# First attention: keys of two blocks by seven products in place of eight

## The chip, the cores and the metric

The kernel runs on one core of a Trainium2 chip. The metric is the device time of one execution in microseconds (us); of several runs the median is taken. The engines are called PE (matrix products), DVE (vector), ACT (activations), POOL (GpSimd) and SP (here only a queue that issues DMAs). PE writes to PSUM, eight banks of 512 columns of fp32 in 128 partitions; everything else lies in SBUF.

## The reference

A network of six layers works on x, 128 rows of 256. The first layer, the only one that the change touches, is an attention of these rows over a context of M = 12544 rows:

```
q = (layernorm(x) @ Wq)           in 4 heads of 64
k, v = context @ Wkv              in 4 heads of 64
attn = softmax(where(mask, q k^T / 8, -inf))
x = x + (attn v) @ Wo
```

Then follow a gated delta net, a layer of experts, a second attention over the same context with 16 heads, a linear attention with decay, and a second layer of experts. All is fp32.

## The kernel before

The context comes transposed, so that its 256 columns lie in the partitions (two halves, index k). It is cut into 24 blocks of 512 rows and a last one of 256 (`BLOCKS`), and each block stays in SBUF in a place of its own (`ctx_blocks[b][:, k, :]`), because the second attention uses it again.

`xattn0_first` (L365) is the first layer. For each block of the context it makes

- keys, transposed (`keys`, L414): kT[:, m, :] for the two halves m of the 256 key columns, each the sum of two products (k = 0, 1) of a 128x128 quarter of Wk with a 128x512 half of the block. So a block takes four products of 128x128 by 128x512. A product in fp32 is two passes of PE, which the profile counts as two instructions;
- values (`values`, L426): eight products with 256 columns;
- scores (`scores`, L449): per 256 rows of the block ("a part"), 16 products into a tile `st` of two banks; DVE adds minus a maximum that was estimated from block 0 (`nm`) and writes `e` (L466), ACT takes the exponential in place (L467), POOL casts the mask to fp32 (`mk`, L469), and POOL, or DVE for the second part of every odd block, multiplies `e` by it (L475);
- `add_up` (L478): DVE adds `e` into `sums`, the denominators;
- `weigh` (L482): PE adds values times `e` into `ot`, which stays in one PSUM bank over the whole layer.

Blocks are taken in pairs (loop at L561). PE's, ACT's and DVE's order is written out by hand (`manual_schedule`); POOL's and SP's is made by a scheduler when the kernel is built. In a pass b > 0 of the loop the order is: values of b-2 and add_up of b-2, values of b-1 and add_up of b-1, keys of b and b+1, weigh of b-2 and b-1, scores of b and b+1. A pair's keys, values and scores go through one ring of three PSUM tiles of two banks each (`two`, L411); `ot` has the seventh bank, and `spare`, into which PE multiplies zeros at the start, has the eighth. `e` has five buffers, the cast masks two.

The scores of the first pair come before that, with the layer norm, the queries and the estimate of the maximum: L541 to L552. While the layer norm waits for other engines, PE makes keys and values of block 0 (`between`).

In the last pass there is one block, 24. `filler` gives PE products of the second attention there (its lines are L1063, keys, and L1084, values), and from then on through the delta net and the experts, so that PE has work while other engines are slow. The filler's total work is fixed.

Weights of later layers are loaded ahead through a ring of four buffers (`ring`, `weights`, L83): Wq, then the four tiles of the delta net's projections in the passes that hold blocks 4, 6, 8 and 10 (`ahead`). All of these loads, the blocks of the context and the masks (L452) are issued on SP's queue.

## Time and profile before

| what | value |
|---|---|
| median of 3 runs | 753.38 us (752.00 to 753.56) |
| the profiled execution | 752.12 us |
| its span, first to last instruction | 750.3 us |
| mean granted clock of PE | 0.993 |
| PE busy in 102.9 to 124.3 us | 21.40 of 21.40 us |
| DVE busy there | 13.06 us |
| ACT busy there | 8.28 us |
| POOL busy there | 10.41 us |
| scores of the first pair on PE | from 20.8 us |
| last weigh of block 23 on PE ends | 271.8 us |

The span is what the profiler shows between the first and the last instruction; the time of the execution is 1.8 us longer. The first attention takes the first 286 us of it. In a group's line stand the source line, the engine, the operation, the tiles written and read (out<-in), the shape and the number of instructions, then the time they were busy in us and the mean of one in ns, then the idle time of the engine just before them and what ended it. A line of the timeline begins with start and length in us; "x4" means four instructions in a row, with their whole length. POOL stands for GpSimd, PEld for PE's loading of weights.

### The profile page before, as it was taken

What the parts mean: (1) busy time and instruction counts of PE and PEld (TensorE: products, weight loads), DVE (VectorE), ACT (ScalarE), POOL (GpSimd) and SP (SyncE); (2) the same over time, 40 slices, a digit from 0 to 9 for tenths busy, and PEclk for the clock granted to TensorE, in tenths of its full rate; (3) what the DMA queues carried; (4) which work ended last, traced back from release to release, by engine and by line L of the source; (5) the groups of instructions that cost most, each with busy time, mean ns of one, the idle gap of its engine ahead of it and who ended that gap; (6) DMA issues with size and microseconds to landing.
All of it is one profiled execution on the core that took longest, in us unless ns stands there. A gap on an engine that the chain in (4) does not pass through costs nothing.

```text
span 750.3 us, 23185 instructions
## 1 busy us (share of the span) xinstructions
PE 733.4 (98%) x10472; PEld 561.4 (75%) x10472; DVE 300.6 (40%) x482; ACT 390.9 (52%) x480; POOL 177.9 (24%) x178
## 2 busy tenths in 40 slices
PE   8999999999999999999999999999999999999985
PEld 4678877777787777666677666668888888888873
DVE  2675556656655555983123251001111111111155
ACT  2434433334344333573235223337789999999931
POOL 5555444455554420506012030000000000000000
PEclk9999999999999999999999999999999999999998
DMA  9980000000000002224111344113652222222000
GB/s 318 385 294 4 9 5 9 8 8 8 8 5 3 1 29 93 94 99 141 46 44 43 126 85 127 74 67 100 158 120 78 69 63 74 74 60 73 6 2 12
DMA packets 36124, 56.66 MB, mean 76 GB/s; under 512 B 5904, under 2 KB 12608, under 8 KB 36016
## 3 DMA queue, kind: packets, MB, share of 16 engines
q1 hardware_dynamic: 35648, 54.05, 23.2%
q8 instruction: 84, 1.38, 0.8%
q0 software_dynamic: 368, 1.03, 0.4%
q14 instruction: 24, 0.20, 0.1%
HBM read 42.09 MB, written 12.98 MB: 73 GB/s over the span
## 4 chain that ended last, share of the span: by engine, by line
PE 92%; ACT 5%; issue 1%; DVE 1%; POOL 0%; ACTq 0%; DVEq 0%; POOLq 0%
PE pv L439 12%; PE pk L1063 11%; PE pv L1084 11%; PE pk L420 11%; PE one L1158 10%; PE st L460 6%; PE ot L489 6%; PE st_a L1143 5%; PE st_b L1143 5%; ACT es L1149 2%; ACT w L1149 2%; PE pr L672 1%; PE one L1143 1%; PE py L992 1%; ACT e L1149 1%
## 5 line engine op out<-in xcount | busy, mean ns | idle before, releaser
L475 POOL TENSOR_TENSOR e<-e,mk 128x1024 f32<-128x1024 f32 x37 | 87.4, 2361 | 130.7 <-issue 116.9
L1143 PE MATMUL one<-qs,ks 32*128 32x128 f32 x784 | 108.1, 282 | 0.0
L1190 DVE TENSOR_TENSOR ctx<-ctx,one 128x512 f32<-128x512 f32 x47 | 32.3, 687 | 163.9 <-PE one L1158 163.9
L1158 PE MATMUL one<-e,ctx 128*17 128x128 f32 x784 | 94.7, 275 | 0.0
L1143 PEld LDWEIGHTS one<-qs,ks 32*128 32x128 f32 x784 | 94.2, 187 | 0.0
L1063 PE MATMUL pk<-ctx,wk 128*128 128x512 f32 (+1 forms) x200 | 92.6, 589 | 0.0
L1084 PE MATMUL pv<-wv,ctx 128*128 128x256 f32 x384 | 90.0, 382 | 0.6 <-ACT kh L1070 0.6
L439 PE MATMUL pv<-wkv,ctx 128*128 128x256 f32 x392 | 88.4, 383 | 0.0
L1084 PEld LDWEIGHTS pv<-wv,ctx 128*128 128x128 f32 x384 | 71.8, 190 | 21.0 <-issue 10.7
L420 PE MATMUL pk<-ctx,wkv 128*128 128x512 f32 (+1 forms) x200 | 86.5, 584 | 0.0
L467 ACT ACTIVATE e<-e 128x1024 f32<-128x1024 f32 x49 | 51.8, 1057 | 64.5 <-DVE e L466 61.1
L439 PEld LDWEIGHTS pv<-wkv,ctx 128*128 128x128 f32 x392 | 73.3, 190 | 10.9
L1158 PEld LDWEIGHTS one<-e,ctx 128*17 128x17 f32 x784 | 73.1, 98 | 6.2 <-issue 0.2
L466 DVE TENSOR_TENSOR e<-st,nm 128x1024 f32<-128x1024 f32 x49 | 56.7, 1218 | 50.1 <-PE st L460 50.1
L1158 PE MATMUL one<-es,ctx 128*17 128x128 f32 x1776 | 74.8, 275 | 0.0
L1149 ACT ACTIVATE es<-st_a 128x1536 f32<-128x1536 f32 x49 | 70.9, 1446 | 0.0
L420 PEld LDWEIGHTS pk<-ctx,wkv 128*128 128x128 f32 x200 | 37.9, 190 | 41.4 <-issue 39.7
L1149 ACT ACTIVATE e<-one 128x512 f32<-128x512 f32 x98 | 58.9, 601 | 17.7 <-PE one L1143 14.9
L1070 ACT ACTIVATE kh<-pk,col 128x512 f32<-128x512 f32 (+1 forms) x50 | 33.8, 678 | 63.7 <-PE pk L1063 62.7
L480 DVE TENSOR_TENSOR sums<-sums,e 128x1024 f32<-128x1024 f32 x49 | 63.1, 1287 | 5.7 <-POOL e L475 3.6
L1158 PEld LDWEIGHTS one<-es,ctx 128*17 128x17 f32 x1776 | 60.5, 98 | 0.1
L1143 PE MATMUL st_a<-qs,ks 32*128 32x128 f32 x1176 | 57.6, 283 | 1.6 <-issue 1.6
(339 smaller groups left out, 1049.7 us busy)
## 6 DMA issues: line engine op xcount, KB each, us to landing
ctx<-in_ctxT SPq DMA_DIRECT2D x24, 512.0 KB, 9.2
kd<-kh SPq DMA_DIRECT2D x48, 256.0 KB, 2.0
ks<-kd SPq DMA_DIRECT2D x192, 64.0 KB, 2.9
w<-in_L_ffn_expert_w SPq DMA_DIRECT2D x4, 512.0 KB, 3.8
ctx<-in_L_ffn_We SPq DMA_DIRECT2D x4, 512.0 KB, 7.2
msk<-in_maskT SPq DMA_DIRECT2D x24, 64.0 KB, 1.9
w<-in_L_attn_Wqk SPq DMA_DIRECT2D x2, 768.0 KB, 10.1
w<-in_L_attn_Wv SPq DMA_DIRECT2D x2, 768.0 KB, 12.0
```

The source lines that it names most:

```text
L420: nc.tensor.matmul(pk[:, m, :n], wkv[:, k, m * 128 : (m + 1) * 128], ctx_blocks[b][:, k, :], start=(k == 0), stop=(k == KC - 1),)
L439: nc.tensor.matmul(pv[:, i, c * D : (c + 1) * D], ctx_blocks[b][:, k, rows], wkv[:, k, D:], start=(k == 0), stop=(k == KC - 1),)
L460: nc.tensor.matmul(st[:, 2 * q + m, c, :], kTs[b][rows, m, (c0 + c) * 128 : (c0 + c + 1) * 128], qT[rows, m, :], start=True, stop=True,)
L466: nc.vector.tensor_add(e, st, nm.unsqueeze(2).to_broadcast([128, 4, 2, S]))
L467: nc.scalar.activation(e, e, AF.Exp)
L475: engine.tensor_mul(e, e, mk.unsqueeze(1).to_broadcast([128, 4, 2, S]))
L480: nc.vector.tensor_add(sums, sums, e)
L1063: nc.tensor.matmul(pk, wk1[:, k, m * 128 : (m + 1) * 128], ctx_blocks[b][:, k, :], start=(k == 0), stop=(k == KC - 1),)
L1084: nc.tensor.matmul(pv[:, c, :], ctx_blocks[b][:, k, rows], wv1[:, k, :], start=(k == 0), stop=(k == KC - 1),)
L1143: nc.tensor.matmul(three[:, j - 1, g, :] if j else one[:, 0, g, :], kss[b % 3][r, g // 2, g % 2, c * 128 : (c + 1) * 128], qs[r, g, :], st ...
L1149: nc.scalar.activation(e.rearrange("p j g s -> p (j g s)"), st.rearrange("p j g s -> p (j g s)"), AF.Exp)
L1158: nc.tensor.matmul(one[32 * j : 32 * j + DH + 1, 0, g, :], v[:, c, 8 * (g // 2) + 2 * j + g % 2, :], e3[:, j - 1, g, :] if j else e1[:, 0, ...
```

## The change

Only `xattn0_first` changes.

Keys of two whole blocks b and b+1 are made together (`seven`), for the eleven pairs from block 2 on. The two blocks are taken as a matrix of quarters a11, a12 (block b, halves k) and a21, a22 (block b+1), Wk as w11, w12, w21, w22; the product of two matrices of two by two quarters is made with seven products of quarters in place of eight, from sums of the quarters. The sums of weights, `tw`, are made once by POOL at the start; the four sums of the context, s1 to s4, are made by POOL for each pair one pass ahead (`add_context`). They lie in two buffers of the ring `ring` and in `places[0]`, two sets in turn. Each of the seven products is one of PE's with its own bank; ACT copies the first into kT of block b, and DVE adds the others to what is there already, SBUF plus PSUM into SBUF, seven adds of 512 columns in all. Keys of blocks 0, 1 and 24 stay as they were.

PSUM is now handed out in single banks: seven in turn (`Banks`), and `ot` in the eighth, zeroed at the very start, where PE's products of zeros also go. So values and keys have a copy for each bank, and the scores of a part have two banks, `st[0]` and `st[1]`, with an add on DVE for each (four heads' halves, 128x512).

The order on PE, ACT and DVE within a pass is written as a string: v is a step of values (four products with 256 columns), k one of the seven products with its copy or adds, a an add into `sums`, m DVE's own mask product, w the weighing of a part, f a step of filler. The mask product of DVE, until now emitted with the scores, thus stands behind a first add.

From POOL's queue as built: in a pass of the steady state POOL has the casts of the first two masks, then the four context sums for the next pass's keys, then mask product, cast, mask product, cast, mask product. At the start it has the weight sums, the conversion of block 0's mask, five DMA issues, the context sums of blocks 2 and 3 and of 4 and 5, among them two small rows (`turned`) and two casts, then the first mask product. On SP's queue the two loads of L0_attn_Wv stand behind the last mask's load now; before, they stood among the loads of the context.

```diff
-            tc.tile_pool(name="x0_mm", bufs=3, space=PSUM) as ps_mm,
+            tc.tile_pool(name="x0_mm", bufs=1, space=PSUM) as ps_mm,
...
+            ot = ot_bank[:, : 2 * S].rearrange("p (m s) -> p m s", m=2)
+            nc.tensor.matmul(ot_bank[:, : 2 * S], zeros[:, :128], zeros[:, : 2 * S], start=True, stop=False)
...
+            tw = wp.tile([128, 4, 128], F32, name="tw")
+            w11, w12, w21, w22 = [wkv[:, k, m * 128 : (m + 1) * 128] for k in range(2) for m in range(2)]
+            nc.gpsimd.tensor_sub(tw[:, 0], w12, w11)
+            nc.gpsimd.tensor_sub(tw[:, 1], w22, tw[:, 0])
+            nc.gpsimd.tensor_sub(tw[:, 2], w22, w12)
+            nc.gpsimd.tensor_sub(tw[:, 3], w21, tw[:, 1])
+            room = [ring.tile([128, 1536], F32, tag="w", name="w") for _ in range(2)]
+            slots = [r[:, i * 512 : (i + 1) * 512] for r in room for i in range(3)]
+            slots += [places[0][:, i * 512 : (i + 1) * 512] for i in range(2)]
...
+            class Banks:
+                def __init__(self, n):
+                    self.left = cycle(range(n))
+                def one(self, name):
+                    i = next(self.left)
+                    return (ps_mm if i else ps_ot).tile([128, 512], F32, tag=f"b{i}", name=name)
...
+            banks, few = Banks(7), Banks(7)
+            next(few.left)
+            def add_context(b):
+                s1, s2, s3, s4 = slots[b // 2 % 2 :: 2]
+                a11, a12 = [ctx_blocks[b][:, k, :] for k in range(2)]
+                a21, a22 = [ctx_blocks[b + 1][:, k, :] for k in range(2)]
+                nc.gpsimd.tensor_add(s1, a21, a22)
+                nc.gpsimd.tensor_sub(s2, s1, a11)
+                nc.gpsimd.tensor_sub(s3, a11, a21)
+                nc.gpsimd.tensor_sub(s4, a12, s2)
+                sums_of[b] = (a11, a12, s4, a22, s1, s2, s3)
+            def seven(b):
+                a11, a12, s4, a22, s1, s2, s3 = sums_of.pop(b)
+                for i in range(2):
+                    kTs[b + i] = kvp.tile([128, 2, 512], F32, tag="kT", name="kT")
+                c11, c12, c21, c22 = [kTs[b + i][:, m, :] for i in range(2) for m in range(2)]
+                for left, right, sums in (
+                    (a11, w11, ()),
+                    (s2, tw[:, 1], ((c12, c11),)),
+                    (a12, w21, ((c11, c11),)),
+                    (s3, tw[:, 2], ((c21, c12),)),
+                    (s1, tw[:, 0], ((c22, c21), (c12, c12))),
+                    (a22, tw[:, 3], ((c21, c21),)),
+                    (s4, w22, ((c12, c12),)),
+                ):
+                    p = banks.one("pk")
+                    nc.tensor.matmul(p, right, left, start=True, stop=True)
+                    if not sums:
+                        nc.scalar.copy(c11, p)
+                    for out, to in sums:
+                        nc.vector.tensor_add(out, to, p)
+                    yield
...
-                    e = ep.tile([128, 4, 2, S], F32, tag="e", name="e")
-                    nc.vector.tensor_add(e, st, nm.unsqueeze(2).to_broadcast([128, 4, 2, S]))
-                    nc.scalar.activation(e, e, AF.Exp)
...
+                st = [banks.one("st").rearrange("p (m c s) -> p m c s", m=2, c=2) for _ in range(2)]
...
+                for q in range(2):
+                    of = slice(2 * q, 2 * q + 2)
+                    nc.vector.tensor_add(
+                        e[:, of], st[q], nm[:, of].unsqueeze(2).to_broadcast([128, 2, 2, S])
+                    )
+                nc.scalar.activation(e, e, AF.Exp)
...
+                if b % 2 == 0 or c0 == 0:
+                    mask(b, c0 // 2)
+            def mask(b, i):
+                engine = nc.vector if b % 2 and i else nc.gpsimd
+                engine.tensor_mul(es[b][i], es[b][i], bys.pop((b, i)))
+            def add_up(e):
+                nc.vector.tensor_add(sums, sums, e)
...
+            add_context(2)
             for b in range(0, NB, 2):
...
-                    for c in (b - 2, b - 1):
-                        if c > 0:
-                            values(c)
-                        add_up(c)
-                    for c in pair:
-                        keys(c)
-                    weigh(b - 2, False)
...
+                    k = seven(b) if len(pair) == 2 else keys(b)
+                    v = chain(values(b - 2) if b > 2 else (), values(b - 1))
+                    order = "v v a0 m3 k k a1 v k k a2 v k k k a3 w0 w1 w2 w3"
+                    if b == 2:
+                        order = "m3 a0 v k k a1 v k k a2 k k k a3 w0 w1 w2 w3"
+                    elif len(pair) == 1:
+                        order = "v v a0 m3 k a1 v k a2 v a3 w0 w1 f f f w2 w3"
+                        filler.into(few, "mm")
...
+                    if b + 3 < NB:
+                        add_context(b + 2)
                 for c in pair:
-                    scores(c)
+                    for c0 in range(0, BLOCKS[c][1] // 128, 2):
+                        scores(c, c0)
```

## The prediction

> **What bounds the kernel now.** I read the busy shares first, then the chain of work in order of time, then the timeline of one period of the first attention, then the groups whose durations I need.
>
> The busy shares of the page:
>
> ```profile
> PE 733.4 (98%) x10472; PEld 561.4 (75%) x10472; DVE 300.6 (40%) x482; ACT 390.9 (52%) x480; POOL 177.9 (24%) x178
> ```
>
> PE is busy in 98% of the span: what it is spared counts, as long as nothing else makes it wait. The chain of work in order of time (start, length, what), one period of the first attention and the start of the next:
>
> ```profile
> 102.98 3.77 PE st L460 x64
> 106.75 7.10 PE pv L439 x32
> 113.86 6.87 PE pk L420 x16
> 120.72 3.65 PE ot L489 x64
> 124.37 3.77 PE st L460 x64
> ```
>
> The period is 3.77 + 7.10 + 6.87 + 3.65 = 21.39 us without a gap. A product of keys is two passes, 6.87 / 16 = 0.43 us each, so 0.86 us. What DVE and POOL do in a period, from the timeline (start, length, engine, line):
>
> ```profile
> 61.35 4.62 DVE L466 TENSOR_TENSOR e<-st,nm 128x1024 f32<-128x1024 f32 x4 [4.59 <-PE st L460]
> 63.80 2.37 POOL L475 TENSOR_TENSOR e<-e,mk 128x1024 f32<-128x1024 f32 x1 [10.71 <-issue]
> 66.26 0.40 POOL L469 TENSOR_SCALAR mk<-msk 128x256 f32<-128x256 uint8 x1
> 66.63 2.36 POOL L475 TENSOR_TENSOR e<-e,mk 128x1024 f32<-128x1024 f32 x1
> 69.07 0.41 POOL L469 TENSOR_SCALAR mk<-msk 128x256 f32<-128x256 uint8 x1
> 69.44 2.35 POOL L475 TENSOR_TENSOR e<-e,mk 128x1024 f32<-128x1024 f32 x1
> 69.51 3.36 DVE L475 TENSOR_TENSOR e<-e,mk 128x1024 f32<-128x1024 f32 x1 [3.54 <-POOL mk L469]
> 71.88 2.59 POOL L469 TENSOR_SCALAR mk<-msk 128x256 f32<-128x256 uint8 x2
> 72.80 5.33 DVE L480 TENSOR_TENSOR sums<-sums,e 128x1024 f32<-128x1024 f32 x4
> ```
>
> Two things are to be seen. DVE's last mask product (69.51) lasts 3.36 us: it starts with POOL's (69.44 to 71.79) and ends 1.08 after it, so it did nothing until POOL was done. Then POOL's two casts take 2.59 in place of 2 x 0.40, while DVE adds up: the two engines take turns, instruction by instruction. But the adds of L466, whose source is a PSUM tile, run at their usual pace while POOL works from 63.80 on. DVE ends at 78.13 and has idle time until the next scores; all of this is hidden now.
>
> Durations that I need, from the groups, from the answer on line 948, and from DVE's timeline in which two instructions follow each other:
>
> ```profile
> L1190 DVE TENSOR_TENSOR ctx<-ctx,one 128x512 f32<-128x512 f32 x47 | 32.3, 687 | 163.9 <-PE one L1158 163.9
> L480 DVE TENSOR_TENSOR sums<-sums,e 128x1024 f32<-128x1024 f32 x49 | 63.1, 1287 | 5.7 <-POOL e L475 3.6
> ```
>
> ```profile
> L948 POOL TENSOR_TENSOR o<-o,sg x3: 1266/1267/1657, 396.8 to 400.4; 128x512 f32<-128x512 f32 x3
> ```
>
> ```profile
> 15.60 0.69 DVE L541 CUSTOM_DVE_ANT_0 t<-sc,mb 128x512 f32<-128x512 f32 x1 [5.11 <-PE sc L538]
> ...
> 16.21 0.69 DVE L541 CUSTOM_DVE_ANT_0 t<-sc,mb 128x512 f32<-128x512 f32 x1
> ```
>
> L1190 has the form of the new key adds (SBUF plus PSUM into SBUF, 512 columns): 0.69 us, and by L541 one starts every 0.61 us.
>
> **The change, part by part.**
>
> *Seven products.* 11 pairs of blocks, one product less each: 0.86 us a pair, 9.4 in all. PE's own work becomes 21.39 - 0.86 = 20.53 a pair. Interleaving values and keys and moving the zeroing product of ot to the start leave PE's sum as it is.
>
> *DVE.* New per pair: 7 key adds, 4.3 us; the four adds of L466 become eight halves (8 x 0.61 = 4.9 for 4.62). ACT loses one copy of 1024 columns and has more, shorter ones; it idles some 13 us a pair, so this is nothing. DVE now stands behind PE: the next scores need the last key add (block b's second half), and the banks come free by DVE's adds. So DVE's order must be walked through.
>
> *POOL.* Four sums of 128x512 per pair. The nearest row is L948, two whole tensors: 1.27 us (L718, of the same width with both inputs broadcast, has a mean of 1.07; L948's mean, with one turn lost to DVE, is 1.40). [...] I take the row.
>
> *Who blocks whom.* [...]
>
> 1. DVE: eight halves to 4.9. The first exp ends at 0.61 + 0.69 + 0.03 + 1.06 = 2.4; POOL's mask of e0 lasts 2.5 to 4.9.
> 2. DVE's first sum (a0) and POOL's cast share 5.0 to 6.4; POOL's mask of e1 to 8.7, its cast to 9.2, the mask of e2 to 11.5. DVE's own mask product needs that cast and, as now, comes second: 11.5 to 12.6. It is a whole sum later than now (72.87 - 61.35 = 11.5), since a0 now comes before it.
> 3. A key add, then the sum a1, 13.3 to 14.3. POOL's first context sum, which asks 0.05 after a1, 14.3 to 15.5 (it holds the lock for 1.13 of its 1.27). Two key adds; the sum a2 asks at 15.63. POOL's second context sum asks at 15.57, so it comes first: a2 waits until 16.7 and ends at 17.8.
> 4. Four key adds, to 20.2; a3 from 20.3 to 21.36. The next pair's half adds start at 21.28.
>
> So a pair takes **21.28 us** in place of 21.39, and PE waits for 0.75 of it, at the second half of the first scores. Of these 21.28, 1.07 is a2's wait. How long PE takes to go on after a DVE add no row shows; I take 0.15, and up to 0.33 it is covered by a3 (20.2 + 0.15 + 0.47 of scores + 0.27 to the first half add = 21.1). [...]
>
> *The first pair (block 2).* Now its period, from the scores' end at 24.6 to the next at 42.5, lasts 17.9 and has room. After: POOL is free of mb at 10.47. Ahead of its first mask it now has one small sum (0.4), five DMA issues (3.45, as now), eight context sums for two pairs (10.2), the two turned rows and two casts (1.2): 25.7, against a start at 24.49 now; with hand-overs 25.9. The chain to the end of DVE's mask product is 9.1 now (24.49 to 33.57), so 35.0. Behind it DVE has a0, a key add, a1, two key adds, a2 and four key adds: 0.26 + 1.07 + 0.61 + 1.15 + 0.26 + 1.22 + 1.15 + 2.44 = 8.2 less overlaps of starts, 7.9: 42.9. Then PE's hand-over, half a score and three more, 3.45: scores end at 46.3 in place of 42.5, and DVE's next pair starts at 44.0 in place of 39.96: **+3.9**. If POOL's sums cost 1.07, +2.4.
>
> *Other steps.* The four weight differences on POOL (some 0.4 each, scaled from L948) run before mb, whose mask lands at 8.5 anyway. The row's diag products may alternate with POOL's sums, up to 0.9 on PE, but the first pair is bound by POOL, so it isn't added. The zeros are ready 0.5 earlier, hidden by the same. Two of the ring's four buffers now hold context sums, so both loads of L0_attn_Wv stand behind all masks on SP's queue until the last seven products are done, near 250, and land 12.0 us later; nothing behind them on SP starts before 269, and their first reader (the fourth projection of delta_net) starts at 313.9. If that cover were gone it would cost up to 12. The last block's pass has the same PE work (15.4) and DVE has time there: 0.
>
> *Sum.* +3.9, and ten pairs at -0.11, -1.1: +2.8. The profiled execution took 752.1 (span 750.3, 1.8 around it); it becomes 754.9. The median of the runs is 1.3 above the profiled one: **756**. The rest of the kernel keeps its order and its work.
>
> **The rivals.** (A) *Faster.* In step 3 POOL's second sum asks only 0.06 us before a2. If a2 comes first, nothing blocks it, DVE needs 20.2 and PE sets 20.53: -0.86 x 10 + 3.9 = -4.7, 748.7. It decides for faster once a pair takes less than 21.0 on average. For it: the margin is a hand-over. Against it: POOL's instructions follow each other at once (66.63 to 68.98, next at 69.07). (B) *Both sums lose.* If POOL's first context sum comes ahead of a1 (margin 0.05), each of a1 and a2 waits a sum: 20.2 + 2.1 = 22.3, ten pairs +9.1, with +3.9: 766.4. (C) *The lock is no matter here*, because adds queue better than the mask product: -8.6 with a first pair of 18 or less, 745. Against it stands the 3.36. That the change doesn't save the product is no rival: 14 passes per pair stand on PE's list.
>
> **How the numbers follow.** Sum as walked 0.45, A 0.23, C 0.02, B and mixtures with it 0.30. 0.2% (1.5 us) is about what a measurement of this kernel can tell. The walked case reaches from 754 to 758, one tenth of all within 0.2%; A and C are faster but for 0.03. So faster 0.25, the same 0.13, slower 0.62. The range takes in A and nearly B: 748 to 765.
>
> **What would show it.** DVE's mask product of 3 us or more, ending 12.6 after the pair's first half add; sums of L480's kind of about 2.2 us beside others of 1.2; idle time of PE ahead of the scores ended by DVE's key add, 0.7 a pair, and 4 at block 2; pairs of 21.3. Wrong: pairs of 20.5 with no waits of PE (A), of 22 and over with two long sums each (B), or a first pair under 20.

## The result, and the profile after

The changed kernel takes 760.31 us (median of 4 runs, 759.22 to 763.10), the kernel before 752.90 us in the same measurement: ratio 1.0105, 95% interval 1.0072 to 1.0138. It is slower, inside the range that was given (748 to 765), and 4.3 us above the predicted 756. The profiled execution took 759.22 us with a span of 757.4 us, 7.1 us more than before.

Busy shares, from the page of the changed kernel:

```profile
PE 727.1 (96%) x10450; PEld 557.7 (74%) x10450; DVE 363.6 (48%) x608; ACT 376.5 (50%) x496; POOL 253.0 (33%) x225
```

PE has 6.3 us less to do (733.4 before) in a span that is 7.1 us longer, so it waits 13 us more. DVE is busy for 63 us more, in which its waits for POOL are counted, and POOL for 75. The chain of work that ended last runs along PE for a smaller part than before; shares of the span by engine, from the two pages (before, then after):

```profile
PE 92%; ACT 5%; issue 1%; DVE 1%; POOL 0%; ACTq 0%; DVEq 0%; POOLq 0%
PE 57%; POOL 20%; ACT 10%; issue 8%; DMA 3%; DVE 1%; SPq 0%; ACTq 0%; POOLq 0%; DVEq 0%
```

One period of the steady state, from the timeline (start, length, engine, line, tiles written and read, shape, count, and in brackets the idle time before and what ended it). The first half add of this period (DVE's add of one half, 128x512, of a part's scores) was at 72.60:

```profile
81.75 2.35 POOL L547 TENSOR_TENSOR e<-e,mk 128x1024 f32<-128x1024 f32 x1
81.82 3.36 DVE L547 TENSOR_TENSOR e<-e,mk 128x1024 f32<-128x1024 f32 x1 [3.12 <-POOL mk L535]
...
85.70 1.21 DVE L550 TENSOR_TENSOR sums<-sums,e 128x1024 f32<-128x1024 f32 x1
85.79 2.26 POOL L452 TENSOR_TENSOR w<-ctx,ctx 128x512 f32<-128x512 f32 x1
...
88.02 1.26 POOL L450 TENSOR_TENSOR w<-ctx 128x512 f32<-128x512 f32 x1
88.03 2.33 DVE L550 TENSOR_TENSOR sums<-sums,e 128x1024 f32<-128x1024 f32 x1
...
89.36 2.15 POOL L451 TENSOR_TENSOR w<-w,ctx 128x512 f32<-128x512 f32 x1
90.28 2.47 DVE L476 TENSOR_TENSOR kT<-kT,pk 128x512 f32<-128x512 f32 x4
91.58 1.27 POOL L453 TENSOR_TENSOR ctx<-ctx,w 128x512 f32<-128x512 f32 x1
...
92.67 1.27 DVE L550 TENSOR_TENSOR sums<-sums,e 128x1024 f32<-128x1024 f32 x1
...
93.86 1.28 DVE L530 TENSOR_TENSOR e<-st,nm 128x512 f32<-128x512 f32 x2
```

DVE's mask product ends at 85.18, 12.58 after the first half add. The add a1 (85.70) asks 0.09 before POOL's first context sum and isn't held up; that sum waits for it (2.26 in place of 1.26). The add a2 asks at 88.03, 0.01 after POOL's second sum (0.01 to 0.03 in the seven pairs from the third to the tenth), and lasts 2.33 in place of 1.21. From there DVE has no gap to the next pair's half adds at 93.86: 21.26 after the last ones.

The next period for PE, the busy times of the engines between two first half adds (length of the stretch, then busy time and instructions of PE, PEld, DVE, ACT, POOL, then PE's granted clock, the DMA share and GB/s):

```profile
93.86:115.11 21.25, 20.80 (x178) 15.86 (x178) 18.14 (x22) 6.86 (x9) 17.38 (x11) 1.00 0.03 8
```

These pairs are a little shorter than before (21.39). The loss lies elsewhere, at the start. There DVE makes four `diag` products, each the identity times minus the maxima of one head; PE multiplies them by ones into `pn`, and DVE copies that into `nm`, which the first scores need. The timeline there:

```profile
17.87 7.75 DVE L607 TENSOR_SCALAR diag<-ident,mx 128x128 f32<-128x128 f32 x4
...
18.45 1.26 POOL L453 TENSOR_TENSOR ctx<-ctx,w 128x512 f32<-128x512 f32 x1
...
24.09 1.25 POOL L453 TENSOR_TENSOR ctx<-ctx,w 128x512 f32<-128x512 f32 x1
...
25.77 2.04 PE L611 MATMUL pn<-diag,ones 128*128 128x512 f32 x2 [6.01 <-DVE diag L607]
27.74 4.28 PEld L523 LDWEIGHTS st<-qT,kT 64*128 64x128 f32 x64 [1.50 <-issue]
27.75 4.48 PE L523 MATMUL st<-qT,kT 64*128 64x128 f32 x64
```

and line L607 by itself (least, median and longest of its four instructions, in ns):

```profile
L607 DVE TENSOR_SCALAR diag<-ident,mx x4: 274/310/7116, 17.9 to 25.4; 128x128 f32<-128x128 f32 x4
```

One of the four diag products, which take 0.28 us each in the kernel before, lasted 7.12 us. It started at 18.31, while POOL was busy, and ended at 25.43, 0.09 after the last of POOL's eight context sums. PE waited 6.01 us for it. PE's granted clock was 0.66 from 20 to 30 us, and 0.89 from 45 to 60, after a second wait, of 3.41 us at block 2. The busy times of three stretches, in the same columns as above, and PE's scores of block 2:

```profile
20.00:30.00 10.00, 4.23 (x30) 2.75 (x32) 6.74 (x4) 0.38 (x1) 5.34 (x6) 0.66 1.05 385
30.00:45.00 15.00, 15.00 (x128) 10.84 (x128) 11.69 (x13) 5.78 (x7) 12.70 (x9) 1.00 0.20 53
45.00:60.00 15.00, 11.42 (x95) 9.49 (x92) 14.25 (x18) 5.88 (x7) 10.99 (x7) 0.89 1.02 377
```

```profile
49.82 4.89 PE L523 MATMUL st<-qT,kT 64*128 64x128 f32 x56 [3.41 <-DVE kT L476]
```

Before, PE was busy throughout at 1.00 in the first and the last of these stretches:

```profile
20.00:30.00 10.00, 10.00 (x88) 7.79 (x87) 5.31 (x5) 6.21 (x6) 5.33 (x4) 1.00 1.05 388
45.00:60.00 15.00, 15.00 (x102) 10.31 (x100) 8.46 (x5) 4.78 (x5) 7.92 (x6) 1.00 0.49 175
```

The two products of pn took 1.02 before and the first scores 3.84, here 2.04 and 4.48.

Where the time goes, by the first half add of each pair's scores (in the kernel before, the first add):

| | before | predicted | after |
|---|---|---|---|
| first pair | 22.03 | 22.03 | 29.57 |
| second pair | 39.96 | 44.0 | 51.08 |
| third pair | 61.35 | 65.2 | 72.60 |
| pairs 3 to 10, each | 21.39 | 21.28 | 21.25 |
| pairs 10 to 12, each | 21.39 | 21.28 | 20.22, 20.53 |
| last block | 273.00 | 275.8 | 281.23 |
| span | 750.3 | 753.1 | 757.4 |

The last block stands for the last part of the layer, block 24. After it the difference of 8.2 grows to 9.1 at the layer's end and falls to 7.1 at the end of the program; why it grows and why some of it comes back was not tried.

### The profile page after: what moved, and what is told of

Read it like the earlier page. It is cut to its first block, busy times and chain, and to the rows that moved or that the text cites. A ratio compares the mean times of both kernels' runs of the same rounds, so it can differ in the third digit from the quotient of the medians.

```text
span 757.4 us, 23376 instructions
## 1 busy us (share of the span) xinstructions
PE 727.1 (96%) x10450; PEld 557.7 (74%) x10450; DVE 363.6 (48%) x608; ACT 376.5 (50%) x496; POOL 253.0 (33%) x225
## 4 chain that ended last, share of the span: by engine, by line
PE 57%; POOL 20%; ACT 10%; issue 8%; DMA 3%; DVE 1%; SPq 0%; ACTq 0%; POOLq 0%; DVEq 0%
PE pk L1139 11%; PE pv L1160 11%; ACT es L1225 8%; POOL e L547 7%; PE one L1234 7%; PE st_a L1219 4%; POOL mk L535 4%; PE st_b L1219 4%; PE pv L501 3%; POOL w L452 2%; POOL w L451 2%; DMA ctx<-in_ctxT 2%; ACT e L1225 2%; PE ot L559 2%; PE st L523 2%
## 5 line engine op out<-in xcount | busy, mean ns | idle before, releaser
L501 PE MATMUL pv<-wkv,ctx 128*128 128x256 f32 x392 | 92.2, 382 | 0.8 <-DVE e L530 0.8
L550 DVE TENSOR_TENSOR sums<-sums,e 128x1024 f32<-128x1024 f32 x49 | 72.4, 1477 | 3.9 <-POOL e L547 3.6
L530 DVE TENSOR_TENSOR e<-st,nm 128x512 f32<-128x512 f32 x98 | 59.8, 679 | 4.9 <-PE st L523 4.7
L523 PE MATMUL st<-qT,kT 64*128 64x128 f32 x784 | 51.5, 285 | 6.4 <-DVE kT L476 6.4
L547 DVE TENSOR_TENSOR e<-e,mk 128x1024 f32<-128x1024 f32 x12 | 40.4, 3365 | 34.8 <-POOL mk L535 34.8
```

Of the source, the lines that this page charges most:

```text
L501: nc.tensor.matmul(pv[:, c * D : (c + 1) * D], ctx_blocks[b][:, k, rows], wkv[:, k, D:], start=(k == 0), stop=(k == KC - 1),)
L523: nc.tensor.matmul(st[q][:, m, c, :], kTs[b][rows, m, (c0 + c) * 128 : (c0 + c + 1) * 128], qT[rows, m, :], start=True, stop=True,)
L530: nc.vector.tensor_add(e[:, of], st[q], nm[:, of].unsqueeze(2).to_broadcast([128, 2, 2, S]))
L547: engine.tensor_mul(es[b][i], es[b][i], bys.pop((b, i)))
L550: nc.vector.tensor_add(sums, sums, e)
```

## The experiments

### The diag products on another engine

```diff
-                nc.vector.tensor_scalar(diag[:, i, :], ident, mx[:, i : i + 1], -1.0, ALU.mult, ALU.mult)
+                nc.scalar.activation(diag[:, i, :], ident, AF.Copy, scale=mx[:, i : i + 1])
...
-            nc.vector.tensor_copy(nm, pn.rearrange("p (h s) -> p h s", h=4))
+            nc.vector.tensor_scalar_mul(nm, pn.rearrange("p (h s) -> p h s", h=4), -1.0)
```

> The changed kernel, with the four diag products at the start made by ACT in place of DVE (and the sign put into DVE's copy of pn). Theory: of the 7.1 us that the whole change costs, about 7 come from one of DVE's diag products, which was shut out by POOL's eight context sums. Then PE's wait at pn falls from 6.0 us to under 1.5, the first half add of the first pair moves from 29.6 to 22.0-22.5, and the time falls by some 4 to 7: 753 to 756. It isn't the full 7, since POOL's context sums still hold the first mask until 25.7, so that the second pair's half adds start near 44-45 (51.1 in the changed kernel). The steady pairs stay at 21.25. Rival: the wait at pn is only the first of two, POOL's queue being the real bound of the start: then the second pair's half adds still start at 49 or later and the time stays at 759 or more.

756.05 us (ratio to before 1.0028, 1.0012 to 1.0043). First half adds at 21.40 and 44.26. The wait at pn is gone; from the timeline of this kernel:

```profile
17.04 1.01 ACT L607 ACTIVATE diag<-ident,mx 128x128 f32<-128x128 f32 x3 [0.82 <-DVE mx L600]
...
19.26 1.02 PE L611 MATMUL pn<-diag,ones 128*128 128x512 f32 x2
...
43.00 6.02 PE L523 MATMUL st<-qT,kT 64*128 64x128 f32 x56 [3.41 <-DVE kT L476]
```

So the shut-out diag product costs 4.3 us of the median. The first scores start 8.2 us earlier, but half of that is lost again, since POOL's queue now holds the first mask. The third line shows what is left: PE waits at block 2 as it was predicted (4 us; here 1.52, then 3.41), and the 56 products of scores behind that wait take 6.02 us, against 3.84 for all 64 where PE doesn't wait; the granted clock is 0.89 from 30 to 45 us and 0.88 from 45 to 60. The next pair takes 22.65 in place of 21.25. That this follows from the slow scores is argued, not tested.

### Is it the form of the instruction?

```diff
-                nc.vector.tensor_scalar(diag[:, i, :], ident, mx[:, i : i + 1], -1.0, ALU.mult, ALU.mult)
+                nc.vector.scalar_tensor_tensor(
+                    diag[:, i, :], ident, -1.0, mx[:, i : i + 1].to_broadcast([128, 128]), ALU.mult, ALU.mult
+                )
```

> The changed kernel, with DVE's four diag products in a form of three operands (ident and the maximum, broadcast along the row, both read from SBUF as tensors) in place of one tensor and a scalar of each partition. Theory: with two tensor inputs from SBUF the product takes turns with POOL's sums, as the adds into sums do: each waits for one POOL instruction at most, the longest of the four lasts 1.5 us or less, PE's wait at pn is 1 to 3 us in place of 6.0, and the time is 754 to 757. Rival: whichever form DVE uses, it is shut out as long as POOL's instructions follow each other without a gap: one of the four lasts some 7 us again and the time stays near 760.

761.28 us (1.0097, 1.0066 to 1.0129); the theory of the form fell, and of the two the rival stood. Line L607 by itself:

```profile
L607 DVE SCALAR_TENSOR_TENSOR diag<-ident,mx x4: 277/278/7162, 18.3 to 25.8; 128x128 f32<-128x128 f32 x4
```

But the rival says too much. In the steady period DVE's a2 waits for one sum, not for the two or three behind it.

### The disputed cost by itself

Three small programs, without the layer's work, measure which engine gets its turn. From the first (`separate` is POOL's row of six adds, `op` is DVE's work, which starts inside the first of them):

```python
        def separate():
            for i in range(6):
                nc.gpsimd.tensor_add(w[i], u, v)
...
            for stream, wait, op in tests:
                nc.gpsimd.tensor_add(head, head, big)
                stream()
                nc.vector.tensor_add(big[:, :wait], head[:, :wait], bank[:, :wait])
                op()
                nc.vector.tensor_add(big[:, 512:], head[:, 512:], bank)
```

> Not a variant of the kernel but the disputed cost by itself: the reference's work is left out altogether. In 14 short tests POOL does six adds of 128x512 (or twelve casts) one behind the other, and DVE starts, inside the first of them, early (0.1 us) or late (0.6 us), one of: four products of ident with a scalar for each partition, 128x128, the diag form; four such products with a third operand added; one add of 128x128, 128x512 or 128x1024. POOL's adds are independent of each other, or each reads the one before, or have both inputs broadcast. Theory 1: POOL gives the lock away only where its next instruction doesn't stand ready (it reads the one before): then every DVE form waits about 7 us behind six independent adds, and one add, 1.3 us, behind dependent ones. Theory 2: short DVE instructions (128 columns) are passed over, long ones not: the diag form and the 128x128 add wait for many, the 128x1024 add for one. Theory 3: DVE, once it has asked, comes next whatever the form, and the 7.1 us have another cause: each waits for one add, 0.6 to 1.3 us.

Theory 3 stood. Behind six independent adds each of four diag products waits for one add:

```profile
L106 DVE TENSOR_SCALAR diag<-ident,head x4: 1197/1296/1297, 6.1 to 9.7; 128x128 f32<-128x128 f32 x4
```

Adds of 128x128, 128x512 and 128x1024, asked for early, last 1.26, 1.67 and 2.20 us, that is the rest of one add of POOL (1.26 us, begun 0.15 before) and their own work; where POOL's adds read each other, two diag products fit into each change (1.20, 0.27, 1.28, 0.27). So here DVE came next after one instruction of POOL, with a diag product as with adds of 128 to 1024 columns. Something in the layer's start must differ. The second program brings in what stands around the products there, one thing at a time (in each test: POOL's row, the size of the add that sets DVE's start, DVE's work, and what is added; `from_mx` is the four diag products):

```python
        tests = [
            (separate, 1, from_mx, ()), (separate, 1, from_mx, ("reduce",)), (separate, 512, from_mx, ("reduce",)),
            (separate, 1, lambda: add(128), ("reduce",)), (separate, 1, lambda: add(1024), ("reduce",)),
            (separate, 1, from_mx, ()),
            (as_in_layer, 1, from_mx, ()), (as_in_layer, 1, from_mx, ("reduce",)),
            (separate, 1, from_mx, ("products",)), (separate, 1, from_mx, ("loads",)),
            (separate, 1, from_mx, ("pool_loads",)), (separate, 512, from_mx, ("pool_loads", "reduce")),
        ]
```

> Again the disputed cost by itself, the reference's work left out. Six independent adds of 128x512 on POOL one behind the other, and DVE's four products in the diag form, which take turns with POOL when nothing else runs (each waits one add, 1.2 to 1.3 us). Now with what stands around them in the layer, one thing at a time: behind two reductions of DVE with an accumulated maximum, from which the scalars come; against POOL's mixture of sums and casts in the layer's order; with PE at work; with eight loads of 512 KB on SP's queue under way; with three loads of 512 KB issued by POOL just before. Theory A: the reduction leaves DVE in a state in which it is passed over: one product lasts 5 us or more in the tests with the reduction, none elsewhere. Theory B: the loads issued by POOL do it: long only with those. Theory C: traffic of any DMA, or PE, does it: long there. Theory D: none of these: 1.3 us everywhere, and the cause of the 7.1 us stays open.

Theory B stood. No diag product lasts over 1.31 us behind the reductions, against POOL's mixture of sums and casts, or with PE at work. In the first test with loads that POOL issued, one lasts

```profile
L142 DVE TENSOR_SCALAR diag<-ident,mx x4: 274/786/6051, 111.3 to 118.6; 128x128 f32<-128x128 f32 x4
```

five adds; in the second such test an add of DVE that came earlier lasted 6.86. The loads on SP's queue had started with the program, ahead of their own test. The first test's two products at 10.3 and 11.4 fell into them (the DMA engines were busy to about 12.8), and waited 1.20 and 1.30 like the others. But where POOL had issued loads, its adds also carried no semaphores (signals to other engines). The third program sets this apart (here `D3` stands for three loads that POOL issues, `head` for one more add ahead of them, `separate` for a row of six adds, `longer` for twelve, `dependent` for six that each read the one before):

```python
        tests = [
            ((), 2, separate, from_mx, ()), ((), 2, separate, lambda: add(128), ()),
            (D3, 1, separate, from_mx, ()), (("head",) + D3, 1, separate, from_mx, ()),
            (("head",) + D3, 1, longer, from_mx, ()), (("head",) + D3, 1, separate, from_mx, ("pause",)),
            (("head", "loads1"), 1, separate, from_mx, ()), (("head",) + D3, 1, separate, lambda: add(1024), ()),
            (("head",) + D3, 1, dependent, from_mx, ()), (("sp",), 2, separate, from_mx, ()),
            (("head",) + D3, 1, separate, lambda: add(128), ()), ((), 2, longer, from_mx, ()),
        ]
```

> The disputed cost by itself once more, the reference's work left out: the diag form (or one add of 128x128 or 128x1024) on DVE against six or twelve adds of 128x512 on POOL. In the run before, a diag product was shut out for 6.05 us, five adds, only in the test in which POOL had just issued three loads; but there POOL's adds also carried no semaphore of their own. Here the two are apart: no loads and no semaphores (two dependent adds ahead of the row); loads with semaphores; loads without; loads with a pause of POOL between them and the row of adds; one load; loads on SP's queue; a row of twelve; a row whose adds read each other. Theory 1: the loads that POOL issued do it: shut out by five adds or more in every test with them, pause or not, and 1.3 us in every test without. Theory 2: the missing semaphores do it: shut out also without loads, and 1.3 us with loads and semaphores. Theory 3: loads do it until POOL has once been idle: 1.3 us in the test with the pause.

Theory 3 stood. The diag products of seven tests, in ns, in this order: no loads and no semaphores; loads with semaphores; loads and a row of twelve adds; loads, and a pause of POOL behind them; one load; loads, and adds that read each other; no loads and a row of twelve:

```profile
L121 DVE TENSOR_SCALAR diag<-ident,mx x4: 1197/1296/1298, 12.7 to 16.3; 128x128 f32<-128x128 f32 x4
L121 DVE TENSOR_SCALAR diag<-ident,mx x4: 274/786/6050, 36.7 to 44.1; 128x128 f32<-128x128 f32 x4
L121 DVE TENSOR_SCALAR diag<-ident,mx x4: 274/786/13361, 67.4 to 82.1; 128x128 f32<-128x128 f32 x4
L121 DVE TENSOR_SCALAR diag<-ident,mx x4: 1196/1297/1298, 93.1 to 96.6; 128x128 f32<-128x128 f32 x4
L121 DVE TENSOR_SCALAR diag<-ident,mx x4: 273/274/7269, 105.7 to 113.3; 128x128 f32<-128x128 f32 x4
L121 DVE TENSOR_SCALAR diag<-ident,mx x4: 273/737/1277, 136.3 to 138.8; 128x128 f32<-128x128 f32 x4
L121 DVE TENSOR_SCALAR diag<-ident,mx x4: 1197/1296/1298, 175.2 to 178.7; 128x128 f32<-128x128 f32 x4
```

With loads issued by POOL ahead of a row of ready adds, DVE waited for five of six, for eleven of twelve, or for all six with one load; an add of 128x1024 lasts 7.05 and one of 128x128 6.12. Semaphores made no difference: the longest product lasts 6.05 with them and without. When POOL had stood still once between the loads and the row (0.80 us), or stood still for 0.08 us between its adds because each reads the one before, DVE got its turn after one add (1.30 and 1.28 us the longest). It is not the transfer itself: the last of the three loads ahead of the row of twelve landed at 70.0, and DVE stayed shut out until 80.7. What in POOL keeps the turn isn't to be seen in these profiles.

In the changed kernel this fits: POOL issues five loads from 10.89 to 14.35, then eight context sums, two rows and two casts follow without a gap to 25.34. But it isn't a strict rule. In the run below with the sums left out from block 6 on, the start has the same loads and the same row; DVE asks at 18.97 in place of 18.31 for the product that has to wait, and it gets two turns within the row. Its four products there:

```profile
L608 DVE TENSOR_SCALAR diag<-ident,mx x4: 274/1240/4094, 19.0 to 25.3; 128x128 f32<-128x128 f32 x4
```

They last 2.03, 0.45, 4.09 and 0.27. When DVE gets a turn within such a row stays open.

### The loads on SP's queue

```diff
-        nc.gpsimd.dma_start(row, a["row"].partition_broadcast(128))
+        nc.sync.dma_start(row, a["row"].partition_broadcast(128))
...
-            nc.gpsimd.dma_start(t, a[name].rearrange("(k p) n -> p k n", p=128))
+            nc.sync.dma_start(t, a[name].rearrange("(k p) n -> p k n", p=128))
```

> The changed kernel with the five loads that POOL issues at the start (row, the router's weights, the second attention's Wk and Wv) issued on SP's queue. Theory: these loads let POOL's instructions that follow shut DVE out; without them the diag products take turns with POOL's sums, none lasts over 1.5 us, PE's wait at pn is under 3 us, the first half adds start at 22 to 25 in place of 29.6, and POOL's sums, 3.5 us earlier, are out of the way of the first mask: 752 to 756. Rival: the row of ready sums does it whoever issues the loads: one diag product lasts 5 us or more, and the time stays at 758 or more, or the contexts' loads, now behind 0.74 MB of others, come late and cost as much.

755.60 us (1.0036, 1.0015 to 1.0058), first half adds at 24.14 and 45.41. Line L607 by itself, with the same sums on POOL behind it and ahead:

```profile
L607 DVE TENSOR_SCALAR diag<-ident,mx x4: 447/692/1302, 18.9 to 21.3; 128x128 f32<-128x128 f32 x4
```

The products take turns with the sums, and PE's wait at pn is 1.15 us. The cost in the kernel is thus shown twice, by the engine of the products and by the issuer of the loads, with nearly the same time. By itself this run doesn't tell whether it is the missing loads: POOL also stands still for 1.63 us ahead of its first sum here, waiting for a block of the context. In the small programs the products took turns behind a row without loads ahead of it and without such a pause (1.30 us the longest).

### POOL's order as in the program

```diff
-            tc.manual_schedule(engines={PE, ACT, DVE}),
+            tc.manual_schedule(engines={PE, ACT, DVE, POOL}),
```

> The changed kernel, diag products on DVE as they are, with POOL's instructions in the order in which the program has them: the context sums of blocks 4 and 5 stand behind the masks of blocks 0 and 1, not ahead of them. Theory: the diag product is shut out as long as POOL's ready work lasts, so until the end of the first pair's fourth sum and one cast, about 20.3 in place of 25.4; PE's wait at pn is about 1 us in place of 6.0, the first half adds start at 23.5 to 24.5 (29.6), the second pair's at 44 to 46 (51.1), and the time is 753 to 757, about as with the diag products on ACT. Rival: the start is late for another reason than the number of sums queued there: second pair's half adds at 49 or later, 759 or more.

778.26 us (1.0315, 1.0293 to 1.0337). First half adds at 23.71 as expected, but not by a shorter shut-out; the second pair's at 47.62, later than expected. POOL stood still for 1.20 us behind its loads, and the diag products took turns with the sums; the timeline of POOL and, after it, line L608 (the diag products here) by itself:

```profile
16.80 0.24 POOL L1196 TENSOR_SCALAR turned<-row 128x8 f32<-128x8 f32 x1 [1.20 <-DMA row<-in_row]
```

```profile
L608 DVE TENSOR_SCALAR diag<-ident,mx x4: 329/876/1301, 18.2 to 20.9; 128x128 f32<-128x128 f32 x4
```

The test with the pause above shows this by itself. That the kernel is 18 us slower than the changed one was in neither theory: the pairs take 23.2 to 23.5. From the timeline of one:

```profile
59.46 1.26 POOL L451 TENSOR_TENSOR w<-ctx 128x512 f32<-128x512 f32 x1
59.53 2.28 DVE L548 TENSOR_TENSOR e<-e,mk 128x1024 f32<-128x1024 f32 x1 [3.11 <-POOL mk L536]
...
62.33 1.70 DVE L551 TENSOR_TENSOR sums<-sums,e 128x1024 f32<-128x1024 f32 x1
...
65.14 2.33 DVE L551 TENSOR_TENSOR sums<-sums,e 128x1024 f32<-128x1024 f32 x1
```

The context sums now begin right behind the cast that DVE's mask product waits for, and three instructions of DVE wait for a sum, not one. The pair's first add (a0, at 53.15) lasts 3.27 as well, beside a mask product of POOL's, and DVE's mask product ends 14.19 after the first half add in place of 12.58. Sums of POOL that come ahead of DVE's instructions, which the prediction's two margins of 0.05 and 0.06 us were about, are met here at three places.

### What sets the steady pair

The sums left out from block 6 on:

```diff
-                nc.gpsimd.tensor_add(s1, a21, a22)
-                nc.gpsimd.tensor_sub(s2, s1, a11)
-                nc.gpsimd.tensor_sub(s3, a11, a21)
-                nc.gpsimd.tensor_sub(s4, a12, s2)
+                if b < 6:
+                    nc.gpsimd.tensor_add(s1, a21, a22)
+                    nc.gpsimd.tensor_sub(s2, s1, a11)
+                    nc.gpsimd.tensor_sub(s3, a11, a21)
+                    nc.gpsimd.tensor_sub(s4, a12, s2)
```

> The changed kernel, with the four context sums on POOL left out from block 6 on: the seven products read the sums of blocks 2 and 4 again, so the keys of blocks 6 to 23 are not those of the reference, with the same work on PE and DVE. Theory: in the steady state DVE's add a2 waits for a context sum and so sets 21.25; without them the pairs from block 6 on are bound by PE at 20.53, first half adds 20.5 apart, and the time falls by 8 pairs x 0.72 = 5.8, to about 754.5. Rival: it is DVE's own larger load (key adds, half adds, the mask product behind a first add) that sets the pair: they stay at 21.1 or more, and the time at 758 or more. The start stays as it is in both.

754.75 us (1.0017, 1.0004 to 1.0030), 5.6 below the changed kernel; first half adds 20.53 apart (the first two pairs 20.39 and 20.28). A period, between two of them:

```profile
91.00:111.52 20.52, 20.52 (x178) 15.79 (x176) 17.05 (x20) 6.95 (x9) 10.49 (x7) 1.00 0.03 8
```

PE is busy throughout. DVE does the same work in 17.05 in place of 18.14; the 1.09 is about a2's wait (2.33 less 1.21). The first pair's half adds are as late as in the changed kernel (29.80). The other way round, eight products with the new banks and order, no sums, no key adds:

```diff
-            def seven(b):
...
-                    k = seven(b) if len(pair) == 2 else keys(b)
+                    k = chain(*(keys(c) for c in pair))
...
-                    order = "v v a0 m3 k k a1 v k k a2 v k k k a3 w0 w1 w2 w3"
+                    order = "v v a0 m3 k k a1 v k k a2 v a3 w0 w1 w2 w3"
```

> The changed kernel's banks, half adds and order, but keys by eight products: no sums of weights and context on POOL, no key adds on DVE. Theory: what costs is POOL's context sums, at the start and in each pair, and not the banks or the order; the pairs take 21.39 again, bound by PE without a wait at the scores, the diag products take their usual 0.2 to 0.3, the first pair's half adds start at 22 to 22.5, and the time is that of the kernel before within 2 us, 751 to 755. Rival: the single banks and the order cost by themselves (more, shorter copies; the mask product behind an add): PE waits ahead of the scores, pairs over 21.6, and 757 or more.

752.01 us (0.9994, 0.9980 to 1.0008), first half adds at 22.65, then 17.93 and 21.39 apart. The banks, the half adds and the mask product behind an add cost nothing here; the loss comes with the sums and the key adds, and in the steady pair, by the run before this one, with the sums.

### Another order on DVE, and both together

```diff
-                    order = "v v a0 m3 k k a1 v k k a2 v k k k a3 w0 w1 w2 w3"
+                    order = "v v a0 k k v k k m3 v a1 k k k a2 w0 w1 a3 w2 w3"
...
-                        order = "m3 a0 v k k a1 v k k a2 k k k a3 w0 w1 w2 w3"
+                        order = "a0 v k k v k k m3 a1 k k k a2 w0 w1 a3 w2 w3"
```

> The changed kernel with another order on DVE in a pass: four of the seven key adds stand between the first add into sums and DVE's mask product, where DVE waits for POOL's cast, and two of the part weighings stand ahead of the last add. Theory: DVE's pair of 21.25 us, made of its own work and a2's wait, sinks below PE's 20.53, for 1.8 us of adds go into time that DVE has idle: first half adds 20.5 apart from block 6 on, and the time falls by 7 x 0.72 = 5, to 754 to 756, with the first two pairs about as before. Rival: the adds only push the mask product back, and POOL's context sums then meet other adds: pairs of 21 or more, 759 or more.

754.88 us (1.0019, 1.0004 to 1.0034), within what was expected, but made up otherwise. The first half adds are 19.87 and 21.5 apart in turn, 20.68 on average, so the seven steady pairs give 3.1 us, not 5. The first two pairs, which were to stay as they were, give 3.6 (19.57 and 19.87 in place of 21.50 and 21.52). The start is unchanged (first pair at 29.85).

With the diag products on ACT as well:

> The changed kernel with both: the diag products on ACT, and the other order on DVE. Theory: the two costs are separate and add up: 4.3 us less by the first (as measured alone) and about 5 by the second, so 750 to 752, below the kernel before by 1 to 3 us. Rival: the low granted clock that follows a wait of PE in the first pairs, or another wait there, takes it back: 753 or more.

747.86 us against 753.40: ratio 0.9925, 0.9899 to 0.9951. This is faster than both kernels, and 2 us more so than expected: the new order also helps the first two pairs (19.78 and 19.95 apart; 22.85 and 22.65 with the diag products moved alone). Its chain by engine, from the page:

```profile
PE 96%; DVE 2%; issue 1%; ACT 0%; POOL 0%; DVEq 0%; ACTq 0%; POOLq 0%
```

Last, POOL's order as in the program on top of both:

> Diag products on ACT, the other order on DVE, and POOL's instructions in the program's order. Theory: with the diag products away from DVE, POOL's queue at the start holds the first mask until 25.3, only some 0.3 us after its first exponential is ready, so the later sums bring nothing more: 746.5 to 749 (747.9 without). Rival: the sums now stand ahead of the first two casts of each pair in place of behind them and meet other adds of DVE: pairs change by 0.3 or more, and the time lies below 746 or above 750.

752.37 us (0.9989, 0.9975 to 1.0002): the rival stood. The pairs take 21.04 in place of 20.68. DVE's mask product and an add each wait for a sum here and last 2.28 us, as in the run with POOL's order alone.

## Why the prediction was right, and where it was not

*Seven products.* Right: PE's own pair is 20.53 without the sums, 21.39 with eight products.

*DVE and the lock.* Right in each step. (The lock is the prediction's word for what its rows show: DVE's mask product lasts 3.36 beside POOL's, and POOL's two casts 2.59 in place of 0.80 beside DVE's adds.) The walk, which counts from the pair's first half add, rests on these rows and on the adds of L466, which read PSUM and kept their pace beside POOL (four in 4.62). Predicted: the mask product ends 12.6 after the first half add, a1 isn't held up, a2 waits for the second context sum by a margin of 0.06, a pair takes 21.28 and PE waits for 0.75 of it. Measured: 12.58; a1 lasts 1.21; a2 lasts 2.33, with a margin of 0.01 to 0.03; 21.25 a pair. PE is idle for 0.45 of it, and its scores, which start twice, last 4.11 in place of 3.84, together 0.72. The trace shows the wait: a2 lasts 2.33 beside a sum that began just before it, and 1.21 in the last two pairs, which have no sums beside them, so it waited for 1.12 of the sum's 1.26 (the sum holds DVE up for 1.13 of 1.27 in the walk). The last four key adds of a pair, which read PSUM, take 2.47 in both cases (2.44 in the walk). With the sums left out the pair takes PE's 20.53, as the prediction has it for DVE without that wait. POOL's sum takes 1.26 to 1.28, the row of 1.27 that was taken. The rivals A and B each needed one of the margins to fall the other way; both fell as walked, in every one of the seven pairs. With margins as small as these, nobody could be sure of that beforehand.

*First pair.* The +3.9 was right in size. In the kernel with the diag products on ACT, where nothing else disturbs it, POOL's first mask starts at 25.25 (25.9 predicted), DVE's mask product ends at 34.30 (35.0), the last key add at 42.95 (42.9), and the second pair starts at 44.26 (44.0). Two small errors cancel there: the mask is 0.7 early, and the add a1 waits for a sum (2.07 in place of 1.21), which the walk didn't have. In the changed kernel itself it is +3.57, and that this is near 3.9 is luck. Everything starts 7.5 later there, so POOL's queue is empty when the first mask is due (2.46 after the first half add, as before), and the cause that was predicted is absent; a1 meets a sum (2.06), and DVE still has its seven key adds to do before PE's next scores, which wait 3.41.

*The failed step* is in "Other steps": "The row's diag products may alternate with POOL's sums, up to 0.9 on PE, but the first pair is bound by POOL, so it isn't added." They did not alternate. One was shut out until POOL's row ended (7.12 us), PE waited 6.0, and the first pair began 7.54 later. The lock was taken as one that DVE, having asked, gets next, which the rows of the kernel before showed; in the changed kernel, behind loads that POOL had issued, it wasn't so. And the cover that was named, POOL's queue, was to hold the first mask until 25.9. As the mask starts 2.46 after the first half add, it covers a half add up to about 23.4; here it came at 29.57. Where the products did alternate, with the loads on SP's queue, PE waited 1.15, near the 0.9 that was named.

*Two smaller terms were missed.* The last two pairs have no context sums beside them any more and take 20.22 and 20.53, 1.8 us less than the sum had for them. And from block 24 to the end of the program another 1.1 come back (0.9 are lost up to the layer's end, then 2.0 gained). Without these the time would have been near 763.

*How far it was luck.* That the kernel is slower follows from what was walked: with the shut-out taken away it still takes 756.05, 0.28% above the kernel before. That this is the predicted number is partly chance, since errors cancel in it. That 760.31 lies inside the range is luck as well. The range reached to 765 for the sake of rival B, which did not come; a cost of 7.5 us that nobody had named took that room. The chances had a slip, too: by the terms given, faster is 0.22 and slower 0.65, not 0.25 and 0.62.

*Right:* the moved weight loads cost nothing (the projections of the delta net wait for no load), and the median stands 1.1 above the profiled execution (1.3 before).

## What to carry to other kernels

Work moved to an idle engine isn't free where a busy one has to wait for it: POOL, busy for 24% of the span before, held up one add of DVE by 1.12 us in each of seven pairs, and one small product by some 6.8 us at the start. So look for each place in which the two meet, the start above all, and not only in the steady state. Here POOL issued loads and then had a long row of ready work; giving what was urgent to another engine than DVE brought 4.3 us, and issuing those loads on another queue 4.7. And walk an order by hand before choosing it: the same seven products were 1.0% slower, 3.2% slower or 0.75% faster than eight, by the order of instructions and the engine of four small ones alone.

## What was not expected of the hardware

- After POOL had issued loads, a diag product or an add of DVE was shut out to the end of POOL's row of ready instructions, or to its last but one: the diag product lasted 7.12 us in the kernel, 6.05 beside a row of six adds, 13.36 beside a row of twelve. In one run DVE got two turns within the row. In the tests without such loads, and in the two in which POOL stood still, for 0.80 us behind the loads or for 0.08 between its adds, a diag product lasted 1.31 us at most; adds of 128 to 1024 columns lasted 1.26 to 2.20 with their own work.
- After a wait of 6.0 us PE's clock was 0.66 in the stretch of 10 us, and pn and the first scores took 1.66 us more than before; after the wait of 3.4 us at block 2 it was 0.89.
